# STU blocks of 126 tokens with both parities in one PSUM bank, a product seeded by ScalarE, a third decay tile, and sums by pairs of units, in a two-layer vision kernel

## The chip, the cores and the metric

The kernel runs on one core of one Trainium2 chip. The metric is the device time of one execution in microseconds (us), the median of several runs. Five engines of the core matter. PE is TensorE, the matrix multiplier; PEld stands for its weight loads. DVE is VectorE, ACT is ScalarE, POOL is GpSimd, and SP is the engine that issues nearly all DMAs here. Each works through its own queue of instructions in order and waits on semaphores for the others. SBUF is the working memory of 128 partitions. PSUM has eight banks of 512 fp32 columns[...].

## The reference

The input is x with 4 images of 48 x 48 tokens and 128 channels, fp32 throughout. Layer 0 is a Mamba-like block: a projection to 256 channels, a 3 x 3 depthwise convolution, and a selective scan in four directions with 16 states a channel. Then attention, then the STU, a bank of spectral filters. The parts that matter here, shortened:

```python
def step(h, inp):                       # layer 0, per direction k
    dt_l, u_l, B_l, C_l = inp
    dA = jnp.exp(dt_l[..., None] * A)
    h = h * dA + (dt_l * u_l)[..., None] * B_l[:, :, None, :]
    y = jnp.einsum('bkdn,bkn->bkd', h, C_l)
    return (h, y)
...
t = t + _L1_attn_ref(_ln_t(t))
t = t + _L1_ffn_ref(_ln_t(t), sigma, phi, M_u, M_phi_plus, M_phi_minus, log_weights, gumbel)
...
def _stu(u, sigma, phi, Mu, Mpp, Mpm):  # layer 1
    # U_plus[t] = sum_s phi[s] u[t-s];  U_minus the same with the sign (-1)^s
    # out = sum_k s_k (U_plus_k Mpp_k + U_minus_k Mpm_k) + sum_{i<3} u[t-i] Mu[i]
...
for i, frac in enumerate((1, 2, 4, 8)): # four STUs on the first T/frac tokens
    outs.append(pad(_stu(x[:, :T // frac], sigma, phi, M_u[i], M_phi_plus[i], M_phi_minus[i])))
out = sum(outs[i] * weights[i])         # weights: a hard choice by log_weights + gumbel
```

Since convolution is linear, the kernel computes the filtered signals once per image and applies, for each token, the sum of the matrices of those STUs whose range the token lies in.

## The kernel before

**Stages.** Image 0 starts with a prologue. Then for every image come the scans of layer 0, and after them the epilogue, the attention and the prologue of the next image. The STU of an image runs *beside the scans of the next image*: PE work of the STU is put between the scans' instructions. Beside the scans of image 0 runs the mixture, which makes the STU's weighted matrices instead. The STU of the last image runs alone at the end. So there is one scan stage with the mixture, three mixed stages of scans and STU, and one lone STU.

**Scans.** `scans` goes through 192 units an image (24 chunks of 384 positions, two channel halves, four groups of states). For one unit, `enter` (L457) multiplies the spread B with dt * u on DVE, or on POOL for three of eight units. Then four times ACT computes a decay tile with an exponential (`dA`, L464) and DVE scans with it (L467). The decay tiles are two PSUM banks, used in turn. POOL then multiplies by C (`times_c`, L476), and two steps later PE sums over states with `sum_c` (L484): four matmuls with 32 columns of weights, each writing another 32 partitions of the bank y. After four such sums DVE adds y to the result (`add_y`). The function `more(share)` takes pieces of STU work until the columns counted as done reach the share of the scans that is issued; the two thus advance in proportion.

**STU.** `stu` cuts 576 positions (2,304 tokens, four residues to a position) into the BLOCKS: lines of (lo, hi, place, extra). For each block it goes through 16 filters; one block and filter is an item, 80 items in all. The convolution is a product with a Toeplitz matrix whose columns are read straight from a table `tt`, which a DMA of overlapping rows fills (L960). The odd and even halves are multiplied in Karatsuba's way with three products c = 0, 1, 2, each for g = 0 and 1: six half products an item, in the order of `convs`. Products c = 0 write bank q0 or q1, products c = 1 write bank c, and products c = 2 accumulate onto the bank of c = 0. The matmuls are in L990; a block that ends at position hi needs one for each 128 positions up to hi.

After a half product `taken` empties the bank. For c = 0 ACT copies it to Q (L1004). For c = 1, g = 0 and g = 1, DVE adds Q and the bank into U (L1019). For c = 2 ACT copies the bank to U (L1016). Each of these is issued just after the matmuls of the next half product (`late`). `project` (L1056) multiplies U of the item before with the mixed matrices G and accumulates in the bank p over the 16 filters; `ar` starts p with the three matrices Mu (L1046). `end` transposes the result (L1073), DVE adds the residual and a DMA stores it.

A block whose tokens lie in the range of a shorter STU in part is handled in two parts (`parts`): the first `extra` positions once with the difference matrix and all w positions once with the common matrix. The mixture makes both kinds of matrix, six to a filter.

**Tables.** `fetch` fills the four slots of `tt` in turn. In blocks 1 and 2 three and two products share a slot; in blocks 3 to 5 each of the three products has a slot of its own. SP issues each load once the matmuls that read the slot before have ended; loads for the scans (`rep`, `bc`) stand in the same queue of SP.

**PSUM.** During the scans: two banks dA, one y, one B (also used by dt and xp), the banks c, q0, q1, and p. That is all eight.

Of the kernel before, what the change touches and what calls it, by code (L numbers as in the profile page):

```python
# [36 lines left out]
BLOCKS = [(0, 128, 0, 72), (128, 256, 2, 16), (256, 384, 4, 32), (384, 512, 5, 0), (512, 576, 5, 0)]  # L37
SHIFT = 55.0

# [15 lines left out]
def hybrid_kernel(ctx: ExitStack, tc: tile.TileContext, a: dict, out: bass.AP):  # L55
# [83 lines left out]
    gd = res.tile([KF, P, 2, 2 * NF - 2, C], F32, name="gd")  # L139
    mud = res.tile([P, 2 * NF - 2, 3, C], F32, name="mud")  # L140
# [296 lines left out]
    class Unit:  # L437
# [21 lines left out]
        def scan(self, g, dAs):  # L459
# [3 lines left out]
            dA = dAs[g % 2]  # L463
# [54 lines left out]
    def scans(b, chunks, preps, front, sp, back, work, work_cols):  # L518
# [40 lines left out]
        dAs = [back.psa.tile([P, 512], F32, tag=f"dA{i}", name=f"dA{b}_{i}") for i in range(2)]  # L559
# [6 lines left out]
        for s in range(len(units) + 2):  # L566
# [3 lines left out]
            if real:  # L570
                units[s].scan(0, dAs)
# [3 lines left out]
            if real:  # L575
                units[s].scan(1, dAs)
# [5 lines left out]
            if real:  # L582
                units[s].scan(2, dAs)
            more((s + 0.75) / len(units))
            prepare(s)
            if real:
                units[s].scan(3, dAs)
# [3 lines left out]
            if s >= 2:  # L591
                units[s - 2].sum_c(back.psy)
                done[0] += CS
                if units[s - 2].q == Q4 - 1:
                    pending.append(units[s - 2])
# [148 lines left out]
    MIX_COLS = KF * 2 * 2 * (6 + 3) * C  # L744
# [3 lines left out]
    def weights(one):  # L748
# [51 lines left out]
        mum = one.tile([P, 2 * NF - 2, 3, C], F32, name="mum")  # L800
        nc.vector.tensor_scalar_mul(mum[:, 5], mu[:, 0], wts[:, 0:1])
        for i in range(1, NF):
            nc.vector.tensor_scalar_mul(mum[:, 6 - 2 * i], mu[:, i], wts[:, i:i + 1])
            if i < NF - 1:
                nc.vector.tensor_tensor(mum[:, 5 - 2 * i], mum[:, 7 - 2 * i], mum[:, 6 - 2 * i], ALU.add)
            yield
# [7 lines left out]
    def mixture(pool, ps):  # L814
# [5 lines left out]

        def keep_(G, p, j, k, q):
            nc.scalar.copy(G[:, :, j], p)
            if j == 0:
                nc.sync.dma_start(gd[k, :, q], G.rearrange("p s j c -> p (s j) c"))

        for k in range(KF):
# [9 lines left out]
            for q in range(2):  # L836
                G = pool.two.tile([P, 3, 2, C], F32, tag="Gm", name=f"Gm{k}_{q}")
                for j in (1, 0):
                    p = ps.psc.tile([P, 3, C], F32, tag=("c", "q0", "q1")[banks[0] % 3], name=f"G{k}_{q}_{j}")
                    banks[0] += 1  # L840
                    for i in range(NF):

                        n = NF - 1 - i if j else 1
                        if i == (NF - 1 if j else 0):
                            continue
                        for t in range(2):
                            nc.tensor.matmul(p[:, :n] if j else p[:, NF - 1 - i], W[:, q if t else 0, i],
                                             M[t][:, i].unsqueeze(1).to_broadcast([P, n, C]) if j else M[t][:, i],
                                             start=(t == 0 and (i == 0 or not j)),
                                             stop=(t == 1 and (i == NF - 2 or not j)))  # L850
                            yield n * C
                    if late:
                        keep_(*late.pop())
                    late.append((G, p, j, k, q))
# [9 lines left out]
    def tail(b, J, T, po, pool, ps):  # L864
# [38 lines left out]
        for j in range(4):  # L903
# [8 lines left out]
                   + (2 * KF + 3) * 4 * (hi - lo + extra) + 4 * (hi - lo) for lo, hi, place, extra in BLOCKS)  # L912

    def stu(b, pool, ps):
# [16 lines left out]
        tts, Gs, Q, U, now, nxt = {}, {}, {}, {}, {}, [0]  # L931
# [3 lines left out]
        convs = [(0, 0), (1, 0), (0, 1), (2, 0), (1, 1), (2, 1)]  # L935

        def do_late(n=0):
# [316 lines left out]
```

## Time and profile before

| What | us |
|---|---|
| Median of 13 runs (6,328.8 to 6,349.3) | 6,342.7 |
| The profiled execution: its time | 6,337.5 |
| The profiled execution: its span, first to last instruction | 6,335.7 |
| PE busy (share of the span) | 5,414.0 (85%) |
| DVE busy | 4,484.0 (71%) |
| ACT busy | 3,051.0 (48%) |
| POOL busy | 3,637.4 (57%) |
| DVE scans, L467: 3,072 of them, mean 0.943 | 2,763.1 |
| PE convolutions, L990: 11,520 passes | 2,503.9 |
| Data moved by DMA | 1,033.6 MB |

The profile is taken from one execution, the trace of which also gives each instruction's start. A matmul of fp32 shows in it as two passes, so counts of PE are twice the counts of the program. The ends of matmuls are modelled: how fast PE goes is read from the distance of the starts of weight loads, not from the durations. A wait is put down to whoever released it last. "Issue" means that the profile shows nothing that was waited for. An average over the span hides that the stages have different limits; they are therefore looked at one by one.

The blocks of an STU can be told apart in the timeline by the transposes at their ends. In the first mixed stage these are at 1,607, 1,807, 2,067, 2,353 and 2,543 us; in the last STU, which runs alone, at 5,730, 5,854, 6,020, 6,213 and 6,331 us.

### The profile page before, as it was taken

To read this page: it belongs to the slowest core of one execution; us is meant where nothing else is said; L and a number is where in the kernel's file an instruction comes from. 1 tells how busy PE (TensorE), PEld (TensorE's weight loads), DVE (VectorE), ACT (ScalarE), POOL (GpSimd) and SP (SyncE) were. 2 spreads that over 40 slices of the span, in tenths; PEclk is the share of its full clock that TensorE was granted. 3 is DMA by queue.
4 is the path that set the end of the run, shared out by engine and by line. 5 is a ranking of instruction groups with operands and counts; after the bars stand their busy time and mean duration, and the time that the engine had idled before them with its cause. 6 is when DMAs were issued, how large, how long until landed. Compare 5 with 4: busy or idle time off the path is not lost.

```text
span 6335.7 us, 76244 instructions
## 1 busy us (share of the span) xinstructions
PE 5414.0 (85%) x25032; PEld 3361.8 (53%) x25032; DVE 4484.0 (71%) x5562; ACT 3051.0 (48%) x6461; POOL 3637.4 (57%) x1825
## 2 busy tenths in 40 slices
PE   3666566788999998789999998789999998889999
PEld 1222222444555667534555667535555666557889
DVE  6998999458889998458889987458889987211000
ACT  2666666245656654246555654246555654222111
POOL 1888888306788887207778886107778877100000
PEclk6777777799999999889999999889999999899999
DMA  4656666127888888127888887137888887025546
GB/s 103 143 141 153 150 146 147 35 63 174 200 210 221 229 221 243 36 67 189 196 214 219 223 230 218 41 80 184 197 210 220 226 225 221 17 74 153 149 143 214
DMA packets 658251, 1033.57 MB, mean 163 GB/s; under 512 B 93856, under 2 KB 515872, under 8 KB 633120
## 3 DMA queue, kind: packets, MB, share of 16 engines
q1 hardware_dynamic: 652032, 1025.00, 62.7%
q10 hardware_dynamic: 5824, 3.69, 0.2%
q8 instruction: 200, 3.28, 0.2%
q14 instruction: 195, 1.60, 0.1%
HBM read 905.79 MB, written 122.56 MB: 162 GB/s over the span
## 4 chain that ended last, share of the span: by engine, by line
PE 52%; DVE 17%; DMA 17%; ACT 4%; POOL 3%; issue 3%; SPq 3%; DVEq 0%; POOLq 0%; ACTq 0%
PE cv L990 24%; DVE s L467 7%; PE pr L1056 7%; DMA tt<-fd 6%; DMA rep<-dtdud 6%; PE y L484 4%; PE s L726 3%; DVE s L457 3%; PE o L719 3%; PE B L448 2%; DMA bc<-xdd 2%; PE op L662 2%; POOL s L476 2%; DVE xc L266 2%; DVE re L414 1%
## 5 line engine op out<-in xcount | busy, mean ns | idle before, releaser
L467 DVE TENSOR_TENSOR_SCAN s<-dA,s 128x385 f32<-128x385 f32 x3072 | 2763.1, 943 | 379.4 <-ACT dA L464 375.5
L476 POOL TENSOR_TENSOR s<-s,bc 128x1536 f32<-128x1536 f32 x768 | 2439.5, 3177 | 199.1 <-DVE s L467 102.8
L464 ACT ACTIVATE dA<-rep,A 128x384 f32<-128x384 f32 x3072 | 1781.6, 585 | 1254.5 <-DVE s L467 1214.2
L990 PE MATMUL cv<-tt,u 128*128 128x256 f32 (+3 forms) x7680 | 1649.5, 354 | 124.2 <-DMA tt<-fd 67.3
L990 PEld LDWEIGHTS cv<-tt,u 128*128 128x128 f32 x7680 | 1272.7, 193 | 639.3 <-issue 303.9
L457 POOL TENSOR_TENSOR s<-rep,bc 128x1536 f32<-128x1536 f32 x288 | 994.0, 3452 | 93.1 <-DMA bc<-xdd 93.1
L457 DVE TENSOR_TENSOR s<-rep,B 128x1536 f32<-128x1536 f32 x480 | 833.5, 1737 | 86.8 <-PE B L448 58.0
L990 PE MATMUL cv<-tt,us 128*128 128x256 f32 (+3 forms) x3840 | 854.4, 351 | 32.0 <-DMA tt<-fd 25.9
L484 PE MATMUL y<-s,csum 128*32 128x384 f32 x6144 | 715.3, 540 | 113.6 <-DVE ya L490 73.0
L990 PEld LDWEIGHTS cv<-tt,us 128*128 128x128 f32 x3840 | 639.9, 192 | 227.7 <-issue 66.4
L1019 DVE TENSOR_TENSOR U<-cv,Q 128x256 f32<-128x256 f32 (+1 forms) x640 | 244.9, 383 | 695.7 <-PE cv L990 686.6
L1056 PE MATMUL pr<-U,G 128*128 128x512 f32 (+4 forms) x2048 | 693.2, 468 | 2.0 <-ACT U L1016 2.0
L448 PE MATMUL B<-xd,spread 128*128 128x384 f32 x960 | 441.8, 545 | 174.1 <-DVE s L457 165.1
L1016 ACT COPY U<-cv 128x256 f32<-128x256 f32 (+1 forms) x640 | 223.4, 349 | 704.6 <-PE cv L990 704.2
L475 POOL COPY carry<-s 128x4 f32<-128x4 f32 x640 | 121.0, 189 | 682.2 <-DVE s L467 644.5
L1056 PEld LDWEIGHTS pr<-U,G 128*128 128x128 f32 x2048 | 335.7, 190 | 193.3 <-issue 140.3
L1004 ACT COPY Q<-cv 128x256 f32<-128x256 f32 (+3 forms) x640 | 223.2, 349 | 380.7 <-PE cv L990 377.3
L726 PE MATMUL s<-xnT 128*128 128x512 f32 (+1 forms) x720 | 357.8, 582 | 42.7 <-ACT xnT L688 23.4
L728 ACT ACTIVATE e<-s,shift 128x512 f32<-128x512 f32 (+1 forms) x360 | 231.2, 644 | 314.0 <-PE s L726 313.6
L484 PEld LDWEIGHTS y<-s,csum 128*32 128x32 f32 x6144 | 126.9, 112 | 467.3 <-issue 317.9
L160 POOL TENSOR_TENSOR ln_vu<-ln_vu,mhalf 128x4 f32<-128x4 f32 (+1 forms) x20 | 26.8, 1340 | 602.1 <-DVE ln_vu L159 602.1
L719 PE MATMUL o<-e,xn 128*128 128x512 f32 (+1 forms) x720 | 343.4, 560 | 4.5 <-ACT e L728 4.5
(161 smaller groups left out, 3769.1 us busy)
## 6 DMA issues: line engine op xcount, KB each, us to landing
rep<-dtdud SPq DMA_DIRECT2D x768, 384.0 KB, 7.6
tt<-fd SPq DMA_DIRECT2D x192, 577.0 KB, 5.2
bc<-xdd SPq DMA_DIRECT2D x2304, 48.0 KB, 3.5
tt<-fd SPq DMA_DIRECT2D x192, 513.0 KB, 4.6
tt<-fd SPq DMA_DIRECT2D x192, 385.0 KB, 4.2
dtdud<-re SPq DMA_DIRECT2D x768, 96.0 KB, 2.2
G<-gd SPq DMA_DIRECT2D x192, 256.0 KB, 5.6
tt<-fd SPq DMA_DIRECT2D x64, 514.0 KB, 5.9
```

The costliest lines, as they stand in the source:

```text
L448: nc.tensor.matmul(self.bt[:, :CS], spread[:, self.ch.k // 2, self.q].rearrange("p c j -> p (c j)"), self.ch.xd, start=True, stop=True)
L457: eng.tensor_tensor(s, self.ch.rep[self.h][:, 1], bt.unsqueeze(1).to_broadcast([P, G4, CS]), ALU.mult)
L464: nc.scalar.activation(dA[:, 1:CS + 1], ch.rep[self.h][:, 0, g], AF.Exp, scale=A[:, ch.k, self.h * G4 + g, self.q:self.q + 1])
L467: nc.vector.tensor_tensor_scan(s, dA[:, CS + 1:0:-1] if ch.rev else dA[:, :CS + 1], s, 0.0, ALU.mult, ALU.add)
L476: nc.gpsimd.tensor_tensor(self.s, self.s, ch.bc[Q4 + self.q].unsqueeze(1).to_broadcast([P, G4, CS]), ALU.mult)
L484: nc.tensor.matmul(ch.y[g * DL:(g + 1) * DL, :CS], csum, self.s[:, g], start=(self.q == 0), stop=(self.q == Q4 - 1))
L719: nc.tensor.matmul(po[J][:, :w], xn[:, i], e[:, :w], start=(i == 0), stop=(i == NT - 1))
L726: nc.tensor.matmul(p[:, :w], xnT[:, i * P:(i + 1) * P], xnT[:, 512 * J:512 * J + w], start=True, stop=True)
L728: nc.scalar.activation(e[:, :w], p[:, :w], AF.Exp, bias=shift)
L990: nc.tensor.matmul(p2[:, :, at - first:], x, t[:, :, hi - 1 - at + J * P:end if end >= 0 else None:-1], start=(c < 2 and J == 0), stop=(J ...
L1019: nc.vector.tensor_tensor(dst, src, q, ALU.add)
L1056: nc.tensor.matmul(p[:, :, :v], Gs[n][:, q, x, :], U[n][:, 4 * q:4 * q + 4, :v], start=False, stop=(k == KF - 1 and q == 1 and v == w))
```

## The change

Seven edits come together.

1. **Blocks of 126.** The blocks end at 126, 252, 378, 504 and 576. A product of one filter then has 4 x 127 = 508 columns at most for both g, and both share one bank. Banks: x for c = 0 and c = 2, y for c = 1. (In the scans y is also the name of a tile of the sums, in another pool.)
2. **Seeding.** No Q is kept. After c = 0 ACT copies bank x to bank y, and the matmuls of c = 1 accumulate onto that copy. The order of products is 0, 2, 1. DVE has no part in the convolution any more. ACT then copies y to U once (504 columns) and x to U in two copies. Once at the start a matmul writes the whole of y (`prime`).
3. **Later.** ACT's copies are issued when 300 more columns of STU work have been issued (`LATER`). U has three buffers, and the projection is that of two items before.
4. **Disjoint segments.** `parts` gives (0, extra) and (extra, w). The mixture makes four matrices to a filter, each already summed, and two banks in place of three are used in turn for it. The projection of an item has one matmul for q = 0 and two for q = 1 in each segment.
5. **Third decay tile.** dA has three banks, the third being one of the two that the STU gives up; the number of banks of the STU falls from four to three.
6. **Sums by pairs.** `sum_c` is called for two units in a row, every second step.
7. **Fetch.** `fetch` is called after a whole product and looks at the next three products.

The core of the diff:

```diff
-BLOCKS = [(0, 128, 0, 72), (128, 256, 2, 16), (256, 384, 4, 32), (384, 512, 5, 0), (512, 576, 5, 0)]
+BLOCKS = [(0, 126, 0, 72), (126, 252, 1, 18), (252, 378, 2, 36), (378, 504, 3, 0), (504, 576, 3, 0)]
+LATER = 300
...
-            dA = dAs[g % 2]
+            dA = dAs[(G4 * i + g) % len(dAs)]
...
-        dAs = [back.psa.tile([P, 512], F32, tag=f"dA{i}", name=f"dA{b}_{i}") for i in range(2)]
+        dAs = [back.psa.tile([P, 512], F32, tag=f"dA{i}", name=f"dA{b}_{i}") for i in range(3)]
...
-            if s >= 2:
+            if s >= 2 and units[s - 2].q % 2:
+                units[s - 3].sum_c(back.psy)
                 units[s - 2].sum_c(back.psy)
-                done[0] += CS
+                done[0] += 2 * CS
...
+                p = ps.psc.tile([P, NF, C], F32, tag=("x", "y")[banks[0] % 2], name=f"G{k}_{q}")
+                for i in range(NF):
+                    n = NF - i
+                    for t in range(2):
+                        nc.tensor.matmul(p[:, :n], W[:, q if t else 0, i],
+                                         M[t][:, i].unsqueeze(1).to_broadcast([P, n, C]),
+                                         start=(t == 0 and i == 0), stop=(t == 1 and i == NF - 1))
...
-        convs = [(0, 0), (1, 0), (0, 1), (2, 0), (1, 1), (2, 1)]
+        seq = [(n, c) for n in range(len(items)) for c in (0, 2, 1)]
+        def do_late(cols=None):
+            if cols is not None and late:
+                late[0][0] -= cols
+            while late and (cols is None or late[0][0] <= 0):
+                late.pop(0)[1]()
...
-            held = next(i for i, (j, cs) in enumerate(order) if j == n and any(c in cs for c, g in left))
+            held = min((place_of[x] for x in seq[:3]), default=0)
             while nxt[0] < min(held + 4, len(order)):
...
+        def prime():
+            for i in range(seeds):
+                p = ps.psc.tile([P, 512], F32, tag="y", name=f"prime{b}_{i}")
+                nc.tensor.matmul(p, ident, u[:, 0], start=True, stop=True)
+        def conv(n, c):
+            w = hi - lo
+            v = w + (c != 1)
+            if c == 0:
+                banks[0] = ps.psc.tile([P, 512], F32, tag="x", name=f"cx{b}_{n}")
+            elif 1 not in banks:
+                do_late()
+            p = banks.pop(1) if c == 1 else banks[0]
+            p4 = p[:, :4 * v].rearrange("p (e m) -> p e m", e=4)
+            for g in range(2):
+                first = lo - (g == 1 and c != 1)
+                for J in range(nb):
+                    at = max(first, J * P) if J else first
+                    x = (sums[:, J, g], u[:, J, 2 + g], u[:, J, g])[c]
+                    nc.tensor.matmul(p4[:, 2 * g:2 * g + 2, v - (hi - at):], x, ...,
+                                     start=(c == 0 and J == 0 and g == 0), ...)
+                    do_late(2 * (hi - at))
+                    if g == 1 and J == nb - 1:
+                        later(lambda: taken(n, c, p, w))
+        def taken(n, c, p, w):
+            if c == 0:
+                U[n] = pool.three.tile([P, 8 * P], F32, tag="U", ...)
+                banks[1] = ps.psc.tile([P, 512], F32, tag="y", name=f"cy{b}_{n}")
+                nc.scalar.copy(banks[1][...], p[...][:, :, 1:])
+            elif c == 1:
+                nc.scalar.copy(U[n][:, 0].rearrange("p g e m -> p (g e m)"), p[:, :4 * w])
+            else:
+                nc.scalar.copy(U[n][:, 1, 0], p[...][:, :, 1:])
+                nc.scalar.copy(U[n][:, 1, 1].rearrange("p e m -> p (e m)"), p[:, 2 * w + 3:4 * w + 3])
...
-            return ((w, 1), (extra, 0)) if extra else ((w, 0),)
+            return ((0, extra, 0), (extra, w, 1)) if extra else ((0, w, 0),)
...
-                    nc.tensor.matmul(p[:, :, :v], Gs[n][:, q, x, :], U[n][:, 4 * q:4 * q + 4, :v], start=False, ...)
+                    if q == 0:
+                        nc.tensor.matmul(p[:, :, :, v0:v1], G, U[n][:, :, :, 0, v0:v1]..., start=False, stop=False)
+                        continue
+                    for g in range(2):
+                        nc.tensor.matmul(p[:, 1 - g, :, v0:v1], G, U[n][:, ::-1 if g else 1, g, 1, v0:v1], ...)
...
+        fetch()
+        prime()
         for n, (_, k) in enumerate(items):
             if k == 0:
                 begin(n)
+            yield from conv(n, 0)
+            fetch()
+            if n > 0:
+                fetch_G(n - 1)
+            if n > 1:
+                if k == 2:
+                    yield from ar(n - 2)
+                yield from project(n - 2)
+            for c in (2, 1):
+                yield from conv(n, c)
+                fetch()
+            if n > 1 and k == 1:
+                do_late()
+                yield from end(n - 2)
```

In the last STU, which runs alone, x and y have two banks each; before, q0, q1 and c had two each.

## The prediction

> **What bounds the kernel now.** I read first the busy times by stage (one row per stretch: microseconds, then busy time and instruction count of PE, PEld, DVE, ACT, POOL, then the granted clock, the DMA engines' busy share and GB/s). The stretches are the scans of image 0, of images 1 to 3 with the STU of the image before beside each, and the last STU alone.
>
> ```profile
> core 0: us, PE busy (x) PEld busy (x) DVE busy (x) ACT busy (x) POOL busy (x), PEclk, DMA share, GB/s
> 105.00:1140.00 1035.00, 617.70 (x2659) 248.17 (x2657) 920.21 (x985) 621.80 (x1276) 873.02 (x423) 0.77 0.61 145
> 1450.00:2543.00 1093.00, 1027.35 (x5315) 655.66 (x5314) 966.08 (x1131) 637.17 (x1393) 871.06 (x421) 0.99 0.84 214
> 2856.00:3959.00 1103.00, 1036.68 (x5314) 661.96 (x5312) 966.59 (x1132) 637.02 (x1392) 871.33 (x421) 0.98 0.83 213
> 4270.00:5376.00 1106.00, 1037.25 (x5320) 661.91 (x5318) 968.60 (x1134) 638.37 (x1395) 871.21 (x421) 0.98 0.83 213
> 5621.00:6331.00 710.00, 697.65 (x3458) 567.80 (x3456) 66.44 (x164) 115.89 (x326) 0.00 (x0) 0.99 0.55 161
> ```
>
> The change touches 5,047 of 6,335.7 us. Image 0's scans hang on DVE, with POOL near it. In the three mixed stages PE (94%), DVE (88%) and the DMA engines (84%) are all nearly full. The last STU is PE alone.
>
> Second, the waits in the first mixed stage (us in total, times, longest):
>
> ```profile
> DVE s L467 <- ACT dA L464: 98.1, 95, 6.6
> PEld y L484 <- issue: 54.0, 139, 0.8
> ...
> PEld cv L990 <- DVE U L1019: 22.4, 17, 4.0
> ...
> PE cv L990 <- DMA tt<-fd: 20.5, 11, 3.8
> ...
> PE cv L990 <- DVE U L1019: 15.4, 13, 3.6
> ```
>
> DVE loses 98 us to decays that are not ready; PE loses 15 us to 38 us waiting for DVE to add Q; filter tables cost 20 us. Third, the pace of PE, since a busy PE is no measure of it. Weight loads in the lone stage:
>
> ```profile
> 5777.97 0.84 PEld L990 LDWEIGHTS cv<-tt,us 128*128 128x128 f32 x4
> 5778.83 0.84 PEld L990 LDWEIGHTS cv<-tt,u 128*128 128x128 f32 x4
> ```
>
> Each matmul instruction appears as two passes. Four passes of 256 columns take 0.86 us, so an instruction costs 1.667 ns a column (0.427 us for 256). Thirty passes of 128 columns in the last block span 3.42 us; hence a floor near 0.213 us an instruction, which I apply to all smaller ones. Last, one visit of the 32-column sums:
>
> ```profile
> 2000.74 0.60 PE L990 MATMUL cv<-tt,u 128*128 128x258 f32 x2
> 2001.27 0.85 PE L484 MATMUL y<-s,csum 128*32 128x384 f32 x8
> 2002.05 0.70 PE L990 MATMUL cv<-tt,u 128*128 128x256 f32 x2
> 2002.59 1.46 PE L990 MATMUL cv<-tt,us 128*128 128x256 f32 x6
> ```
>
> The convolution before ends its columns at 2000.74 + 0.43 = 2001.17; the one after starts streaming at about 2002.16. The visit takes 0.99 us, of which four column tiles side by side need 2 x 384 columns = 0.64: 0.35 us is entering and leaving.
>
> [...]
>
> **Part by part: PE columns.** All per STU, 16 items a block.
> - Block 1: convolutions 1,540 to 1,516 columns; projections 2 x (288 + 512) columns, 2.67 us, to 288 + 216 + 2 x (144 + 108), 1.75 us with the floor: -0.96 us an item, -15.4.
> - Block 2: convolutions -0.12 us; projections 2.13 to 2.08, since 36 and 72 columns pay the floor: -2.8.
> - Block 3: -0.20 and 2.13 to 1.87: -7.5. Block 4: -0.28 and -0.03: -4.9.
> - Block 5 grows from 64 to 72: convolutions 6.41 to 7.05, projections 0.85 to 0.96: +11.9.
> - AR start 14.2 to 11.8: -2.4.
>
> Sum -21 us. By the transposes' times the blocks of the lone stage last about 90, 123, 165, 193 and 119 us, 690 in all; new about 669.
>
> **Sums by pairs.** 192 visits become 96: -34 us of PE a stage. The older unit is only summed one step later. Its s buffer is one of six and is wanted again no earlier than two steps after the sum. y gains a step between add_y and the next start, so the small PE wait for it goes.
>
> **DVE, ACT.** The additions of Q go:
>
> ```profile
> L1019 DVE TENSOR_TENSOR U<-cv,Q 128x256 f32<-128x256 f32 x127 | 51.2, 403 | 7.1 <-PE cv L990 6.7
> ...
> L1019 DVE TENSOR_TENSOR U<-cv,Q 128x128 f32<-128x128 f32 x32 | 8.7, 272 | 6.7 <-PE cv L990 6.6
> ```
>
> DVE falls from 966 to 906 us a stage. ACT had four copies an item at 0.37; now two of 504 at about 0.58 (512 take 0.586) and two of 252: +0.4 us x 64, with block 5 +30 us a stage. ACT goes from 58% to about 65%: hidden. The seed goes PSUM to PSUM, not in the trace; I take 0.58, bounds 0.4 and 0.8.
>
> **Third dA tile.** ACT may run one more scan (0.88 us) ahead. It can save at most 42 waits x 0.88 = 37 of the 70 us that DVE waits for dA in image 0's scans; I take 28, bounds 0 and 45. In the mixed stages it shortens the times when PE, which also waits for DVE, is held: -25, bounds 0 and 50.
>
> **New waits.** (a) x is one bank, so the next item's first product waits for two U copies (0.74 us plus queue on ACT). Behind it on PE stand B, dt and y for the scan. Its cover is the second product, 0.84 us in block 1 and at least 1.67 later. I charge 16 x 1 us in block 1, bounds 0 and 40. The third product waits for the seed, but a projection (0.96 to 2.08 us) stands between: nothing. (b) Tables. In blocks 3 to 5 each product has its own of four slots. The table for c=2 of the next item takes the slot of c=1, free only at the end of the item; PE wants it after one product and one projection: 5.0 us in block 4, 2.35 + 0.96 = 3.3 us in block 5. Before, the shortest lead was four half products and a projection, 5.1 us in block 5. The loads need, from issue to landing:
>
> ```profile
> tt<-fd SPq DMA_DIRECT2D x192, 577.0 KB, 5.2
> ...
> tt<-fd SPq DMA_DIRECT2D x192, 513.0 KB, 4.6
> ```
>
> In a mixed stage scan work stretches 3.3 to about 5.2 us, yet SP issues this load only once PE is through, with bc and rep loads queued behind it in SP. I charge 32 us a stage beyond today's 20, bounds 0 and 90. In the lone stage an unhindered load lands nearer 4 us: 16 x 0.6 = 10, bounds 0 and 30.
>
> **Mixture.** 81,920 columns instead of 73,728, 32 copies instead of 64, two banks for three: PE is 60% busy there: nothing, bounds -5 and +10.
>
> **The sum.** Scan work on PE in a mixed stage: y 192 x 0.99, B 120 x 0.64, dt 48 x 0.64, xp about 20: 318 us. PE needs 690 + 318 = 1,008 of 1,093: 85 are lost. Then it needs 669 + 284 = 953, above DVE's 906 and POOL's 871. Losses: 85 - 38 (DVE's additions) - 25 (third tile) + 16 + 32 = 70. Stage 1,023, -70. Total: 3 x -70, lone stage -21 + 10 = -11, image 0 -28: -249. Span 6,335.7 - 249 = 6,087. That execution took 6,337.5 and the median of 13 is 6,342.7, 7 above the span: **6,094 us**.
>
> **Rivals.**
> - Other bounds hold the mixed stages. For: the stage moved 234 MB, and 250 GB/s, the best over 100 us here, allows 936 us; POOL needs 871; the last blocks run at a DMA share of 0.9. Against: PE's share is higher still. If 30 us a stage and 15 elsewhere are won: 6,342.7 - 105 = 6,238.
> - Losses shrink: third tile, third U and later copies decouple the engines, leaving 25 us over PE's 953. 3 x -115, image 0 -45, lone stage -20: 5,933.
> - Slower: table leads. Without its 106 us charge the change wins 355. Blocks 3 to 5 have 48 items in four STUs, 192. A stall of 1.85 us an item eats everything; at 2.5 us (+480) it is 6,468. For it: loads take up to 11.9 us in the last block. Against: most land in five to six, and block 4 leads by 5.0 us of PE time or more.
> - It doesn't do what it says: seeds or x hold PE so that the additions' waits only change their name, and tables stall too: no net gain, near 6,343.
>
> **How the numbers follow.** Forecast 0.55 (alone 6,030 to 6,160), other bounds 0.19, small losses 0.18, slower 0.06, nothing 0.02. To leave out no more than two in ten the range takes in half of each neighbour: 5,930 to 6,250. Faster by over 0.2% (what a measurement of this kernel can tell) 0.92, within 0.02, slower 0.06.
>
> **What would show it.** Right: mixed stages near 1,023 us, DVE busy near 906 in them, DVE's wait for dA far below 98, PE's waits now on DMA tt and on ACT's copies, the lone stage near 700, its first block near 73 and last near 140. Wrong: PE waiting for tables over 90 us a stage, or the mixed stages standing still while PE falls below 90% busy.

## The result, and the profile after

| | before | after |
|---|---|---|
| median, us | 6,343.6 (44 runs) | 6,320.4 (10 runs, 6,314.7 to 6,327.7) |
| ratio, 95% interval | | 0.9965 (0.9957 to 0.9973) |
| span of the profiled execution | 6,335.7 | 6,319.0 |
| image 0's scans, first scan to last | 1,015 | 995 |
| mixed stages 1, 2, 3, first scan to last | 1,106, 1,116, 1,116 | 1,124, 1,121, 1,123.5 |
| lone STU, first convolution to last | 700 | 679 |

The change wins 23 us where 249 were forecast. Image 0's scans and the lone STU each won about 20 us. The three mixed stages, where a gain of 210 us was expected, grew by 10 each on average. (Stage lengths are from here on taken from the starts of a stage's first and last scan, or of the lone STU's first and last convolution. Before the change the mixed stages are so 10 to 13 us longer than in the windows of the prediction.)

Busy times by stage of the kernel after, in the columns of the prediction's first view; the mixed stages are whole here:

```profile
core 0: us, PE busy (x) PEld busy (x) DVE busy (x) ACT busy (x) POOL busy (x), PEclk, DMA share, GB/s
105.00:1134.00 1029.00, 607.78 (x2441) 239.29 (x2440) 925.67 (x995) 609.24 (x1248) 881.15 (x428) 0.76 0.61 145
1419.50:2543.50 1124.00, 1003.68 (x5600) 725.31 (x5600) 927.72 (x983) 648.22 (x1402) 873.13 (x422) 0.96 0.84 210
2842.80:3963.70 1120.90, 1003.80 (x5605) 726.45 (x5608) 928.84 (x983) 648.12 (x1402) 872.78 (x422) 0.96 0.83 211
4262.90:5386.50 1123.60, 1011.34 (x5605) 732.48 (x5608) 927.72 (x983) 647.53 (x1402) 873.18 (x422) 0.96 0.83 210
5605.00:6315.00 710.00, 692.82 (x3754) 611.29 (x3752) 9.14 (x21) 141.80 (x333) 1.01 (x1) 0.99 0.54 160
```

The whole mixed stages before, for comparison:

```profile
1442.70:2548.50 1105.80, 1034.15 (x5348) 660.08 (x5352) 975.06 (x1143) 641.79 (x1402) 874.22 (x422) 0.98 0.84 214
2849.10:3965.00 1115.90, 1043.27 (x5348) 666.23 (x5352) 975.19 (x1143) 641.86 (x1402) 874.49 (x422) 0.97 0.83 212
4265.60:5381.70 1116.10, 1041.69 (x5348) 664.62 (x5352) 975.51 (x1143) 642.07 (x1402) 874.38 (x422) 0.98 0.83 212
```

In the first mixed stage DVE fell from 975 to 928 us, 47 of the 60 that were forecast, and PE from 1,034 to 1,004. Both are busy for less time, and the stage is no shorter: each of the two now stands idle for longer. PE is busy 89% of the stage; "the mixed stages standing still while PE falls below 90% busy" was one of the prediction's own signs of being wrong. DMA moves 210 GB/s, not 214, at the same share of 0.84. Which waits fill the idle time is in the waits of this stage from 1,444 to 2,538 us, a stretch as long as the prediction's (engine, line, releaser: us in total, times, longest):

```profile
ACT U L1021 <- PE cx L1002: 183.4, 65, 10.6
...
DVE s L468 <- ACT dA L465: 138.6, 105, 3.6
...
ACT cy L1016 <- PE cx L1002: 81.0, 55, 4.2
ACT U L1019 <- PE cy L1002: 70.2, 54, 4.0
...
PE cx L1002 <- DMA tt<-fd: 46.8, 18, 7.6
POOL s L477 <- DMA bc<-xdd: 39.0, 11, 6.4
...
DVE s L458 <- PE B L449: 34.6, 12, 9.4
PE B L449 <- DVE s L458: 31.3, 17, 3.3
...
PE pr L1061 <- DMA G<-gd: 23.9, 6, 7.7
```

Before, ACT's waits for PE and PE's wait for B, in the prediction's window, were these:

```profile
ACT U L1016 <- PE cv L990: 115.8, 91, 6.9
...
ACT Q L1004 <- PE cv L990: 35.7, 33, 4.2
...
PE B L448 <- DVE s L457: 8.8, 8, 2.1
```

The additions are gone from DVE, and with them PE's wait for them (15 us). But ACT's copies now wait 335 us for PE instead of 152, and ACT works in order: the exponentials that stand behind a waiting copy can't start. (One case in the trace after: ACT waits 2.68 us for PE until its copy to y starts at 2,023.53 us, the exponential behind it starts at 2,024.01, and DVE's next scan, which has waited 1.98 us for it, at 2,024.63.) DVE waits 139 us for dA, not the 98 of before, in spite of a third tile, and PE in turn waits 31 us, not 9, for the bank B that DVE reads. All of PE's waits for DVE, added up over the first mixed stage, are 40 us before and 39 after. What grew for PE are its waits for loads: tables cost it 47 us instead of 20, and the matrices G, which are not among its waits before, 24.

### The profile page after: what moved, and what is told of

It is laid out like the page before. It is cut to its first block, busy times and chain, and to the rows that moved or that the text cites. A ratio compares the mean times of both kernels' runs of the same rounds, so it can differ in the third digit from the quotient of the medians.

```text
span 6319.0 us, 76717 instructions
## 1 busy us (share of the span) xinstructions
PE 5275.5 (83%) x25810; PEld 3578.7 (57%) x25810; DVE 4279.1 (68%) x4927; ACT 3075.7 (49%) x6429; POOL 3633.4 (58%) x1825
## 4 chain that ended last, share of the span: by engine, by line
PE 48%; DMA 20%; DVE 19%; ACT 6%; issue 3%; SPq 3%; POOL 2%; ACTq 0%; DVEq 0%; POOLq 0%
PE cx L1002 15%; DVE s L468 8%; PE cy L1002 8%; DMA tt<-fd 6%; DMA rep<-dtdud 6%; DVE s L458 4%; PE y L485 4%; DMA G<-gd 4%; PE s L728 3%; PE o L721 3%; PE pr L1065 3%; DMA bc<-xdd 2%; PE pr L1061 2%; PE B L449 2%; PE op L664 2%
## 5 line engine op out<-in xcount | busy, mean ns | idle before, releaser
L1002 PE MATMUL cx<-tt,u 128*128 128x254 f32 (+7 forms) x3840 | 842.2, 363 | 135.3 <-DMA tt<-fd 127.2
L1002 PEld LDWEIGHTS cx<-tt,u 128*128 128x128 f32 x3840 | 677.3, 201 | 306.8 <-issue 135.1
L1002 PE MATMUL cx<-tt,us 128*128 128x254 f32 (+7 forms) x3840 | 793.1, 348 | 13.7 <-DMA tt<-fd 13.7
L1002 PE MATMUL cy<-tt,u 128*128 128x252 f32 (+5 forms) x3840 | 783.7, 347 | 0.0
L1002 PEld LDWEIGHTS cx<-tt,us 128*128 128x128 f32 x3840 | 646.9, 190 | 159.1 <-issue 47.9
L1002 PEld LDWEIGHTS cy<-tt,u 128*128 128x128 f32 x3840 | 649.6, 191 | 124.1 <-issue 37.0
L485 PE MATMUL y<-s,csum 128*32 128x384 f32 x6144 | 642.9, 539 | 36.8 <-POOL s L477 26.1
L1021 ACT COPY U<-cx 128x252 f32<-128x252 f32 (+1 forms) x320 | 112.1, 350 | 842.7 <-PE cx L1002 840.5
L449 PEld LDWEIGHTS B<-xd,spread 128*128 128x128 f32 x960 | 179.0, 206 | 379.7 <-DVE s L458 320.9
L1061 PE MATMUL pr<-U,G 128*128 128x288 f32 (+6 forms) x1024 | 321.7, 427 | 74.7 <-DMA G<-gd 74.3
```

Source lines behind the costliest of these rows:

```text
L449: nc.tensor.matmul(self.bt[:, :CS], spread[:, self.ch.k // 2, self.q].rearrange("p c j -> p (c j)"), self.ch.xd, start=True, stop=True)
L485: nc.tensor.matmul(ch.y[g * DL:(g + 1) * DL, :CS], csum, self.s[:, g], start=(self.q == 0), stop=(self.q == Q4 - 1))
L1002: nc.tensor.matmul(p4[:, 2 * g:2 * g + 2, v - (hi - at):], x, t[:, :, hi - 1 - at + J * P:end if end >= 0 else None:-1], start=(c == 0 and ...
L1061: nc.tensor.matmul(p[:, :, :, v0:v1], G, U[n][:, :, :, 0, v0:v1].rearrange("p c g m -> p g c m"), start=False, stop=False)
```

## The experiments

Four theories of where the 80 us a mixed stage went (forecast -70, measured +10) were set against one another; the expectations call them by these letters.

- **A, late loads.** Tables and G are asked for too late; the time of issue is at fault.
- **B, backlog.** The DMA engines have too much to move in the mixed stages; the bytes are at fault.
- **C, ACT's queue.** Copies that wait for PE hold the decays behind them.
- **D, a floor of the scans.** DVE and POOL can't go through a scan stage in much less than 990 us.

Each ratio is to runs of the kernel before on the same chip at the same time. The stage lengths are those of the one profiled execution, which can lie off the median: 6,150.2 against 6,169.1 us in e15_ahead1, 6,210.9 against 6,200.8 in e6_later. Differences of 2 or 3 us a stage are therefore not read.

| label | kernel | median, us | ratio to before (95%) | image 0 | mixed, mean | lone |
|---|---|---|---|---|---|---|
| | before | 6,343.6 | | 1,015 | 1,113 | 700 |
| | after | 6,320.4 | 0.9965 (0.9957–0.9973) | 995 | 1,123 | 679 |
| e1_order | after, slots in order of use | 6,271.3 | 0.9871 (0.9853–0.9889) | 990 | 1,102 | 679 |
| e5_order_G | e1, G an item earlier | 6,209.7 | 0.9784 (0.9765–0.9804) | 993 | 1,087 | 674.5 |
| e6_later | e5, copies issued later | 6,200.8 | 0.9772 (0.9753–0.9791) | 991 | 1,086 | 673 |
| e9_lag | e6, tables a product later | 6,196.9 | 0.9782 (0.9768–0.9797) | 997.5 | 1,086 | 674 |
| e2_after_notab | after, four table loads an image | 6,107.1 | 0.9614 (0.9599–0.9630) | 991.5 | 1,052 | 674 |
| e3_before_notab | before, the same | 6,244.4 | 0.9831 (0.9816–0.9846) | 1,015.5 | 1,080 | 700 |
| e7_before_pairs | before, sums by pairs | 6,315.6 | 0.9957 (0.9941–0.9973) | 1,012 | 1,104 | 701 |
| e12_segments | before, disjoint segments | 6,305.5 | 0.9946 (0.9931–0.9961) | 1,016 | 1,108 | 676 |
| e14_before_notab_ps | e3, pairs and segments | 6,155.7 | 0.9696 (0.9680–0.9712) | 1,021 | 1,058 | 672 |
| e8_dA2 | after, two decay tiles | 6,357.7 | 1.0013 (1.0004–1.0022) | 1,025 | 1,124 | 679 |
| e4_dve2 | after, two copies on DVE | 6,356.0 | 1.0005 (0.9995–1.0015) | 994 | 1,139 | 678 |
| e10_nocopy | e5, no copies | 6,119.7 | 0.9658 (0.9642–0.9674) | 986 | 1,057 | 672 |
| e13_nocopy_notab | e10, four table loads | 5,886.2 | 0.9273 (0.9259–0.9287) | 990.5 | 978 | 671 |
| e11_serial | after, STU behind the scans | 7,817.6 | 1.2333 (1.2315–1.2352) | 993 | 937 | 677 |
| e15_ahead1 | e6, decays one scan ahead | 6,169.1 | 0.9714 (0.9695–0.9732) | 989 | 1,068 | 674.5 |
| e16_ahead2 | e6, decays two scans ahead | 6,209.7 | 0.9784 (0.9769–0.9799) | 1,039 | 1,072 | 675 |

### The loads: when they are issued

**e1_order.** In blocks 3 to 5 the three tables of an item are loaded in the order of use 0, 2, 1, so that a table takes the slot that came free first.

```diff
             m = min(3, SLOT // (2 * (hi + 1)))
+            if m == 1:
+                return [range(0, 1), range(2, 3), range(1, 2)]
```

> The changed kernel, but in blocks 3 to 5 the tables take their slots in the order in which they are used (0, 2, 1), so that the table for the third product is loaded one and a half items earlier; same bytes, same matmuls. Theory A, tables come too late: PE's wait for tt (47 us in the first mixed stage) falls below 15 and each mixed stage loses 30 to 60 us, so the time is 6,150 to 6,240. Theory B, the DMA engines as a whole are the limit: DMA share stays at 0.84 and the time within 15 us of the changed kernel. Theory C, ACT's copies that wait for PE hold up the decays behind them: within 20 us of the changed kernel.

Measured: 21 us a mixed stage. Before this edit PE's waits in the whole span were 141 us for tables and 74 for G. With it they are:

```profile
PE pr L1063 <- DMA G<-gd: 96.2, 30, 7.3
...
PE cx L1004 <- DMA tt<-fd: 28.8, 11, 4.6
```

The tables have shrunk to 29 us, and the second late load stands out. In the kernel before the change, G was asked for after the first half product of an item and used after the third of the next: by the starts of the lone stage's items (5,649.65 and 5,654.95 us) 5.30 + 2 x 0.43 = 6.2 us ahead. In the changed kernel it is asked for one item ahead, and an item of block 1 has become shorter (5,677.49 to 5,681.85 us): 4.4 us. G takes 5.5 us to land (median of the 192 loads in the changed kernel).

**e5_order_G.** G is fetched an item earlier, once the projection has freed its buffer.

```diff
-            if n > 0:
-                fetch_G(n - 1)
             if n > 1:
                 ...
                 yield from project(n - 2)
+            fetch_G(n)
```

> As the run with the tables in order of use, and the matrices G of an item are loaded right after the projection that frees their slot, two items ahead of their use in place of one; same bytes. Theory A (loads are asked for too late): PE's 96 us of waits for G go, the mixed stages (first to last scan, 1,098 to 1,105 us there) fall by 15 to 30 us each, time 6,180 to 6,230. Theory B (the DMA engines' total is the limit): stages stay within 8 us, time 6,250 to 6,290. Theory C (ACT's copies hold up the decays): little, 6,245 to 6,280.

Another 15 us a stage. The waits for G go, but tables cost PE 76 us of the span again, where e1 had 29. **e9_lag** goes the other way with the tables: it holds back each load by one product, so that SP is not blocked ahead of the scans' loads (in the first mixed stage of the changed kernel SP waits 161 us for PE before it can issue table loads).

```diff
-            held = min((place_of[x] for x in seq[:3]), default=0)
+            held = min((place_of[x] for x in last[-1:] + seq[:3 - len(last[-1:])]), default=0)
```

> The kernel with tables in order of use, G two items ahead and later copies; and each table load is issued one product later, so that SP does not stand waiting for the product that PE has just been given, with the loads of bc and rep behind it. If SP's head-of-line waits are what makes bc late (POOL waits 139 us for bc over the span in the run without this), those waits halve and the mixed stages (1,083 to 1,088 us, first to last scan) fall by 8 to 20 us each, time 6,140 to 6,185. If the DMA engines' backlog makes them late, nothing changes, or tables come later again and the time rises by up to 40 us.

Nothing is won that can be told. POOL's waits for bc fall from 139 us in e6 (whole span) to 89, but PE's for tables rise from 57 to 97, as the two kernels' waits show; first those of e6_later:

```profile
POOL s L477 <- DMA bc<-xdd: 138.9, 51, 6.2
...
PE cx L1004 <- DMA tt<-fd: 57.1, 24, 6.5
```

and those of e9_lag:

```profile
PE cx L1006 <- DMA tt<-fd: 96.9, 48, 5.8
...
POOL s L477 <- DMA bc<-xdd: 89.3, 34, 6.4
```

The lateness is handed from one to the other. Theory A holds for 36 us a stage. In e5 PE still waits 26 to 35 us a stage for loads, as long as before the change; an issue still earlier than e5's was not tried.

### The loads: how much they move

**e2_after_notab** and **e3_before_notab** load the tables for the first four slots alone and read these again for all later ones, so what they compute is the STU with other filters. In both kernels:

```diff
-                t = pool.four.tile([P, SLOT], F32, tag="tt", ...)
+                if nxt[0] < 4:
+                    full[nxt[0]] = pool.four.tile([P, SLOT], F32, tag="tt", ...)
+                    nc.sync.dma_start(full[nxt[0]]..., ...)
+                t = full[nxt[0] % 4][...]
```

> The changed kernel with the filter tables loaded for the first four slots only, and these read by all items; the output is then that of other filters. All other loads stay. Theory A: waits for tt are zero, stages lose 40 to 60 us, time near 6,170. Theory B: a third of the bytes is gone, DMA share falls to about 0.5 and the stages come down to 960 to 1,010 us, time 5,980 to 6,060; waits for G and bc go as well. Theory C: stages lose less than 25 us, time 6,250 or more.

> The kernel before with the same cut of the table loads; output of other filters. Theory A: the 20 us of waits for tt in a stage go, time near 6,280. Theory B: stages fall to between 1,020 and 1,050 us, time 6,130 to 6,210. Theory C: near 6,280 or more.

Before wins 33 us a mixed stage, after 71, waits for G included, which go as well. So the price of the tables rose by 38 us a stage with the change. The earlier issue of e1 and e5 (A) gives 36 of the 71 back. The other half went only with the bytes: e5 still stands at 1,087 and e2 at 1,052, with a DMA share of 0.59 instead of 0.88. Theory B has a part, though less than its forecasts (960 to 1,010 for e2, 1,020 to 1,050 for e3), and these runs don't tell whether the bytes themselves are at fault or a lead that the four slots don't allow.

### Parts of the change alone

**e7_before_pairs** has the sums by pairs alone (edit 6), **e12_segments** the segments alone (edit 4, on blocks of 128), **e14_before_notab_ps** both, with the tables' loads left out as in e3.

```diff
-            if s >= 2:
+            if s >= 2 and units[s - 2].q % 2:
+                units[s - 3].sum_c(back.psy)
                 units[s - 2].sum_c(back.psy)
-                done[0] += CS
+                done[0] += 2 * CS
...
-            return ((w, 1), (extra, 0)) if extra else ((w, 0),)
+            return ((0, extra, 0), (extra, w, 1)) if extra else ((0, w, 0),)
```

> The kernel before with the sums by pairs of units alone. If the prediction's 0.35 us for entering and leaving the 32-column mode is right and PE sets the pace of the mixed stages, each of them falls by 20 to 34 us and the time by 60 to 100 us. If PE does not set the pace, a stage falls by less than 10 us and the time by less than 30. Image 0's scans do not move by more than 8 us either way.

> The kernel before with the disjoint segments alone (four matrices to a filter, one matmul per segment; blocks of 128, Q and all else as before). PE has 28 us less to do per STU: -0.96 us an item in block 1, -0.21 in block 2, -0.43 in block 3, and -2 for the start. The lone STU falls by 25 to 28 us in any case. If PE sets the pace of the mixed stages they fall by 20 to 28 each, time near 6,240; by theory D by 0 to 10 each, time 6,290 to 6,330.

> The kernel before, tables loaded for the first four slots only, with sums by pairs and disjoint segments; output of other filters. Without tables the kernel before has mixed stages of 1,078 to 1,083 us. PE has 34 + 28 = 62 us less to do in a stage. If the DMA backlog is what swallowed these savings before (14 us of 62 came through), the stages fall by 45 to 62 us, to about 1,025. If the coupling by ACT's and DVE's queues swallows them, they fall by less than 25.

Pairs win 9 us a mixed stage, segments 5 there and 24 in the lone one, both together 22 without the tables, of 62 that PE has less to do by the prediction's prices. So it is not the tables alone that swallow the saving. The saving on PE itself is real. A visit for two units, in the timeline of PE after (start, duration, instruction):

```profile
2000.38 1.01 PE L1002 MATMUL cx<-tt,us 128*128 128x252 f32 x4
2001.32 1.50 PE L485 MATMUL y<-s,csum 128*32 128x384 f32 x16
2002.75 2.38 PE L1002 MATMUL cx<-tt,us 128*128 128x252 f32 x10
```

The convolution ends its columns about 2 x 0.42 us after 2000.38 (252 columns at the prediction's 1.667 ns), at 2001.22, and the next begins at about 2002.8: 1.6 us for two units, where two single visits took 1.98: 0.38 less, near the 0.35 that the prediction put on entering and leaving. That PE needs 34 us less doesn't make the stage 34 us shorter.

**e8_dA2** is the changed kernel with two decay tiles.

```diff
-        dAs = [... for i in range(3)]
+        dAs = [... for i in range(2)]
```

> The changed kernel with two decay tiles as before. By the prediction's terms: image 0's scans back from 995 to about 1,015 us, mixed stages 25 us longer each, time near 6,415. If the third tile is worth nothing in the mixed stages: image 0's 20 us alone, time near 6,340.

The third tile is worth 30 us in image 0's scans (1,025 to 995), and nothing that can be told in the mixed ones (1,124 to 1,123). With two tiles image 0's scans take 10 us more than before the change; what in the rest of it costs them was not looked into.

### How fast the scans can be

**e11_serial** puts the STU behind the scans of each image, not beside them.

```diff
-            scans(b, *first, front, sp, ps, stu_alone(b - 1, ps, 1), STU_COLS)
+            scans(b, *first, front, sp, ps, iter(()), 0)
+            for _ in stu_alone(b - 1, ps, 1):
+                pass
```

> The changed kernel with nothing beside the scans of images 1 to 3: each STU runs alone after them. Same work. Shown by it: how long scans take by themselves with PE free. The prediction took DVE's 906 us of busy time as their floor, so 910 to 940 us from first to last scan. Theory D: 960 to 1,000 us, as with the mixture beside them. The whole is then 7,850 to 8,050 us, each STU about 680.

The scans alone take 937 us, with DVE full:

```profile
1450.00:2350.00 900.00, 474.81 (x1828) 131.12 (x1826) 882.12 (x940) 532.80 (x1035) 836.69 (x406) 0.66 0.56 134
```

DVE is busy 882 of 900 us, so theory D falls: the floor is 937, below PE's 953. The mixed stages lie 186 us above it.

### ACT's queue

**e4_dve2** gives the two copies of bank x to U to DVE.

```diff
-                nc.scalar.copy(U[n][:, 1, 0], ...)
-                nc.scalar.copy(U[n][:, 1, 1]..., ...)
+                nc.vector.tensor_copy(U[n][:, 1, 0], ...)
+                nc.vector.tensor_copy(U[n][:, 1, 1]..., ...)
```

> The changed kernel with the two copies of the third product on DVE in place of ACT. Theory C: of ACT's 335 us of waiting for PE in a mixed stage the 183 us for these copies leave ACT's queue; if they were what delays the decays, DVE's wait for dA falls from 139 us to below 70 and the time by 60 us or more. Theories A and B: DVE now waits for PE itself (100 us or more a stage) and the time is equal or up to 60 us longer than that of the changed kernel.

Worse by 16 us a stage. The waits in the stretch 1,450 to 2,450:

```profile
ACT U L1019 <- PE cy L1002: 168.8, 55, 11.9
...
DVE s L468 <- ACT dA L465: 84.2, 69, 3.3
...
DVE U L1021 <- PE cx L1002: 17.4, 19, 3.5
```

DVE's wait for dA did fall, from 131 us in the same stretch of the changed kernel to 84, but not below 70, and the time didn't fall at all. ACT's next copy, that of y, waits 169 us in place of 62. DVE has 62 us more to do a stage (the two copies take 248 over four STUs), and itself waits 17 for PE. The run doesn't tell these apart. **e6_later** leaves the copies on ACT and issues them later in blocks with long products.

```diff
-            late.append([LATER, f])
+            late.append([max(LATER, cols), f])      # cols: 0.6 of the product's columns, for c = 1 and 2
```

> The kernel of the run before in this call, and ACT's copies of the third and second product are issued only when 60% of the next product's columns are issued, where that is more than 300 columns. Theory C: ACT then finds PE done more often, its waits for PE and DVE's for dA (about 490 us over the span) fall by a fifth or more, and the time falls by 20 us or more against that run. If the copies are not what holds the decays: within 12 us, or up to 30 us slower since x is freed later.

Nothing that can be told, where theory C had said 20 us or more: ACT's waits for PE fell from some 320 us a stage to 281, DVE's for ACT only from 137 to 123. **e10_nocopy** has none of the copies: no seed, and the projection reads one constant U. **e13_nocopy_notab** has neither the copies nor the tables' loads.

```diff
-                nc.scalar.copy(banks[1]..., p...[:, :, 1:])
...
-                nc.scalar.copy(U[n][:, 0]..., p[:, :4 * w])
...
-                nc.scalar.copy(U[n][:, 1, 0], ...)
-                nc.scalar.copy(U[n][:, 1, 1]..., ...)
```

> The kernel with tables in order of use and G two items ahead, without ACT's four copies per item: no seed, no copy to U, the projection reads one constant U; matmuls and loads stay. The output is not the STU's. Theory C (ACT's copies hold up the decays, and PE waits for the banks): mixed stages fall from 1,087 to 1,040 us or less, time below 6,080. Theory D (the scans' own chain of DVE, ACT and POOL sets a floor near 990 us, and what is above it is mutual waiting for PE and for loads): stages stay above 1,065, time above 6,140. By the prediction's bound, PE at 953 us: about 1,000.

> Both cuts together on the kernel with tables in order of use and G two items ahead: no copies by ACT, and tables loaded for the first four slots only; output of other values. If DMA backlog (1,087 to about 1,051 without the tables' bytes) and ACT's copies (to 1,057) are two separate losses, the mixed stages come to about 1,020 us. If they feed each other and nothing else holds, they come to PE's demand of 953 plus a little: 965 to 1,000. If a third limit stands behind both, they stay above 1,035.

From e5's 1,087, taking the copies away gives 1,057 (-30, between what theory C, 1,040 or less, and theory D, over 1,065, had said), taking the tables' bytes away 1,052 (-35, by e2, where PE hardly waits for a load any more), and both 978 (-109): more than the two together. Each loss hides more than half of the other: the copies are worth 30 with the loads there and 74 without them. PE waiting for banks that ACT has not emptied is not what the copies cost: PE's own waits for ACT are 2 to 8 us a stage in the changed kernel and in e5. In e13 the stage is PE's, and DVE hardly waits for dA at all; busy times and that wait in the stretch 1,450 to 2,450:

```profile
1450.00:2450.00 1000.00, 973.85 (x5607) 718.56 (x5606) 913.24 (x1000) 545.72 (x1055) 860.49 (x419) 0.98 0.60 144
```

```profile
DVE s L468 <- ACT dA L465: 12.0, 12, 2.5
```

PE is busy 97%, and 978 is 25 us above the 953 that the prediction worked out for it.

**e15_ahead1** keeps all work and alters ACT's order: each exponential is issued one scan earlier, ahead of the copies that would stand before it. **e16_ahead2** issues it two earlier.

```diff
-        def scan(self, g, i, dAs):
+        def decay(self, g, i, dAs):
...
+        def run_scan(s, g):
+            units[s].scan(g, s, dAs)
+            while ahead[0] < min(G4 * s + g + 1 + 1, G4 * len(units)):
+                i, j = divmod(ahead[0], G4)
+                units[i].decay(j, i, dAs)
+                ahead[0] += 1
```

> The kernel with tables in order, G two items ahead and later copies; each decay is issued on ACT one scan earlier, before the STU's copies that used to stand in front of it. All work stays. If the order in ACT's queue holds the mixed stages, DVE's waits for dA (430 us over the span) fall by a third or more and the stages (1,083 to 1,088) fall by 10 to 25 us each, time 6,130 to 6,175. If it only shows up as a wait and PE or DMA is the limit, within 15 us of that kernel (6,201).

> The same with the decays two scans earlier, as far as three tiles allow. If the order in ACT's queue holds the stages: another 5 to 15 us a stage below the run with one. A decay then waits for the scan before last to end, with the STU's copies behind it: if that delays PE's banks, the time is up to 40 us longer than with one.

One ahead wins 18 us a mixed stage over e6 in the profiled executions, which are the fastest of e15 and the slowest of e6; by the medians it is 32 us in all, near 11 a stage. DVE's wait for dA in the stretch 1,450 to 2,450 is 106 us in e6:

```profile
ACT dA L465 <- DVE s L468: 144.6, 161, 3.7
DVE s L468 <- ACT dA L465: 106.3, 69, 4.5
ACT cy L1018 <- PE cx L1004: 101.2, 52, 7.0
...
ACT U L1023 <- PE cx L1004: 71.2, 42, 7.8
...
ACT U L1021 <- PE cy L1004: 49.3, 33, 8.4
```

and 24 in e15, with 18 more for ACT's copy of the carried state, while the copies for the STU still wait 169 us for PE:

```profile
ACT dA L463 <- DVE s L472: 194.0, 231, 6.9
POOL s L481 <- DMA bc<-xdd: 74.1, 27, 6.3
ACT cy L1034 <- PE cx L1020: 71.8, 44, 4.9
ACT U L1039 <- PE cx L1020: 56.4, 36, 6.4
...
ACT U L1037 <- PE cy L1020: 40.4, 26, 9.8
...
DVE s L472 <- ACT dA L463: 23.6, 20, 3.5
...
DVE s L472 <- ACT s L470: 17.6, 22, 2.9
```

That supports theory C in part: with all copies still there and only the order altered, some of the loss goes, so what stands behind a waiting copy counts. But the copies' waits fell too (222 to 169), and 32 us is less than half of the 81 that leaving the copies out wins over e6. Two ahead is no better in the mixed stages and loses 50 us in image 0's scans; why was not looked into. e15 is the fastest kernel that does the whole work, 0.9714 of before and 151 us below the changed kernel's median. Its mixed stages are still 115 us above PE's 953. ACT's exponentials now wait 194 us for a free tile, so they are well ahead; the next largest wait is POOL's for the loads of bc, at a DMA share of 0.90 and 225 GB/s:

```profile
1450.00:2450.00 1000.00, 930.91 (x5239) 670.84 (x5236) 887.74 (x925) 619.34 (x1313) 825.19 (x401) 0.98 0.90 225
```

How the 115 us divide between the DMA engines and ACT was not settled.

## Why the prediction was wrong, point by point

The difference of the mixed stages can be followed through five kernels that differ by one step each: before 1,113, without tables 1,080, with pairs and segments 1,058 (e14), with the rest of the change 1,052 (e2), with tables again 1,123 (after).

| step | forecast, us a mixed stage | measured, us a mixed stage |
|---|---|---|
| on PE: segments -28, pairs -34 | -62 | 1,058 - 1,080 = -22 |
| blocks of 126 on PE +7, additions -38, third tile -25, bank x +16 | -40 | 1,052 - 1,058 = -6 |
| tables and G | +32 | (1,123 - 1,052) - (1,113 - 1,080) = +38 |
| sum | -70 | +10 |

(The -28 for the segments is that of e12's expectation; with +7 for the blocks it makes the prediction's -21.) The order in which parts are taken away has a share in these numbers, since they don't add.

- **The step that failed** is the sum of losses, "85 - 38 (DVE's additions) - 25 (third tile) + 16 + 32 = 70", put on top of a PE that needs 953. It held PE to be the bound, so that a microsecond less on PE is one less of the stage, and held a wait that goes to be time won. In stage lengths taken the same way, before loses 1,113 - 1,008 = 105, and after 1,123 - 953 = 170. In a mixed stage before the change, pairs and segments bring 14 one by one (9 and 5), and with the tables gone 22 together, of the 62 that PE has less to do by the forecast. Nor did waits go: PE waits for DVE 40 us before and 39 after.
- **The -38 for the additions** was, besides, read too high. It adds the wait of PE (15) and that of its weight loads (22) for the same additions; in the trace all 13 of PE's stalls fall on stalls of the weight loads, so PE itself lost 15.
- **"ACT goes from 58% to about 65%: hidden"** was the blind spot in it. The added time was right: ACT's copies took 447 us before (four STUs) and 567 after, 30 an STU, though ACT's busy share of a mixed stage stayed at 58%. But the cost of a copy isn't its duration. A copy that waits for PE holds the decays behind it, DVE waits for these, and PE for DVE: that is the reading of the waits, and e13 and e15 support it. The last rival had said that "the additions' waits only change their name, and tables stall too: no net gain". It had 0.02, and in this it was what happened, but not by its cause: seeds or x do not hold PE, whose waits for ACT come to 2 or 3 us a stage. So the 16 us for bank x were not needed either.
- **Third dA tile.** 28 forecast for image 0's scans, 30 measured by e8; the stage won only 20, since the rest of the change costs it 10, the upper bound that the prediction gave to the mixture. In the mixed stages 25 forecast, 1 measured. There DVE waits for ACT about 150 us with two tiles (e8) as with three, so a free tile was not what the decays lacked.
- **Tables.** 32 charged, and with G 38 measured: near, but partly by luck, since the lead of G was not looked at. Earlier issue takes back 36: 21 by order (e1), and 15 by G (e5). The rows of the first block's tables are 508 bytes instead of 516: a packet of 508 bytes took 27 ns in the median and 41 in the mean, one of 516 before 28 and 41.
- **The lone STU.** -21 in columns came in (700 to 679; e12 gives 24 from the segments alone). The 10 us charged for stalls did not: PE waits for tables 4.4 us there.
- **The seed.** 0.58 us taken for ACT's copy of 504 columns from PSUM to PSUM; the trace has a mean of 0.559. The changed kernel has one matmul write the whole of each bank y at the start of an STU (L980, at 1,418.43 us for the first) and then seeds 80 products an STU; no run leaves that matmul out and keeps the seeds, so whether they need it was not shown. No wait of PE's third product for the seed stands in the first mixed stage: it was rightly put at nothing there.
- **Other bounds.** The rival with -30 a stage had part of the mechanism, the DMA engines, but not its size: bytes alone don't hold the stage (e10 with all tables runs it in 1,057), nor do ACT's copies alone (e2, 1,052). PE's 953 was near what e13 reached (978), as a floor, and wrong as the base of a forecast.

## What to carry to other kernels

Where, as here, two engines and the DMA queues are all above 80% and a third is near it (in the first mixed stage PE 89%, DVE 83%, DMA 84%, POOL 78%), don't subtract a wait from the stage: ask of each instruction that is moved to another engine what it will wait for there and what stands behind it in that engine's order, and issue the work that others wait for ahead of it. Here a saving on the busiest engine counted in full only where it ran alone (21 of 21 us in the lone STU, 22 of 62 in a mixed stage without the tables). When a loop is made shorter, every load that is asked for a fixed number of steps ahead loses lead (here G in block 1: 6.2 to 4.4 us, with 5.5 to land), so look up each one's landing time, not only the one of the buffer that was touched.

## What the runs showed of the hardware

- Loads came late well before the DMA engines' share was full. At 0.88 and 219 GB/s (e5, 1,450 to 2,450) POOL waited 42 us for bc, and at 0.59 and 139 GB/s, without the tables (e2), 0.2. Taking away the tables' bytes won 35 us a stage by itself, and 79 once ACT's copies were gone as well (1,057 to 978).
- A copy by ACT of 504 columns from PSUM to PSUM took no longer than one to SBUF: means of 559 and 579 ns in the changed kernel.
- PE's granted clock in the scans was 0.66 where they ran alone (e11, 1,450 to 2,350 us), 0.97 or 0.98 with the STU beside them before the change and 0.96 after it (the whole mixed stages).
